# A hand-written schedule with shifted priorities: 207 parts of a four-layer network on one core

## The chip, the core and the metric

The kernel runs on one core of a Trainium2 chip. A core has four compute engines that each work through their own instruction list in order: PE (matrix multiplies, with its weight loads shown as PEld), DVE (vector work), ACT (activation functions and copies) and POOL (general vector work). SP here only issues DMA transfers. The engines run beside each other and wait for one another by semaphores. PE reads its operands from the on-chip memory SBUF and writes into PSUM[...].

The metric is the device time of one execution in microseconds (us). Shown are the median of three runs, and one profiled execution with its trace.

## What is computed

An input of 8 sequences x 256 tokens x 128 channels goes through six blocks, each with a normalisation in front and a residual sum behind:

```python
x = x + 0.5 * soft_moe(layernorm(x))
x = x + linear_attention(layernorm(x))
x = x + 0.5 * soft_moe(layernorm(x))       # the same weights
x = x + 0.5 * ternary_glu(layernorm(x))
x = x + favor_attention(layernorm(x))
x = x + 0.5 * ternary_glu(layernorm(x))    # the same weights
```

The soft mixture of experts (16 experts, 64 slots each, hidden width 256):

```python
logits   = einsum("bnd,esd->bnes", layernorm(x), slot_keys)
dispatch = softmax(logits, axis=tokens)
combine  = softmax(logits, axis=all_slots)
slots    = einsum("bnd,bnes->besd", layernorm(x), dispatch)
hidden   = gelu(slots @ Wg + bg) * (slots @ Wu + bu)
out      = einsum("bns,bso->bno", combine, hidden @ Wd + bd)
```

Linear attention has 16 heads of 8 channels with elu(x)+1 features; the favor attention has the same heads with 32 random exponential features. The glu block has silu(w1 x) * (w2 x) with width 512, then two 512 x 512 layers with gelu, then a projection back to 128. All numbers are float32.

## The kernel before

The eight sequences (called batches b) are split into two groups of four. Each group passes through the six blocks: dispatch for its four batches, 16 experts over all four batches at once, combine and linear attention for each batch, a second dispatch, experts and combine, then a glu for each pair of batches, favor attention for each batch, and a glu for each pair again, which stores the result.

Nothing is issued in that order. `macaron_kernel` first only describes the work: every call of `step` (many hundreds of them) adds a `Step` with a length in ns on each engine that could do it, the buffers and cells that it reads and writes, and a closure that issues the instructions. `Plan.place` (L97) then puts the steps in order with a small model: it takes again and again the step that can start first, over all engines that it may use; ties are broken by `s.key` (L136). A step can start when its inputs are done (plus a lag for the engine that made them), its engine is free, and there are free slots for the buffers that it is the first to use. `issue` (L168) runs the closures by the starts found. From then on each engine's list is fixed; on the chip only the semaphores count, and a step that comes late holds up all that stands behind it on its engine.

The key is the sum of the PE lengths of the steps described so far in a group (L86); the second group starts at 45,000 ns (`BEHIND`, L201). So of two steps that could start at once, the one nearer to the front of its group's work goes first, with the second group 45 us behind:

```python
late = self.TABLE if s.table and s.table != table else 0
rank = (at, s.key + 4 * late, s.number)
```

`late` is the time of loading another function table on ACT (exp, gelu or silu); a step that needs one is ranked behind others.

The places that are spoken of later:

- `normalized` (L348): statistics on DVE (L361, L362), the root on POOL (L367, L368), the subtraction and scaling on POOL or DVE (L374).
- `transposed` (L394): turns a tile on PE (L331), brought out of PSUM by a copy (L338 on ACT, L340 on DVE) or with gain and bias (L416 on ACT, L418 on DVE).
- `dispatch` (L498): four steps of logits (L511), copied to the buffer `comb`, with a running maximum on DVE (L528). Then for each half of the slots a token softmax: maximum on DVE (L542), exp with its sum on ACT (L550), reciprocal on DVE (L558), division on POOL (L563), turned on PE, and gathered into the slots (L584). Last, for the combine softmax: the maximum over slots (L603, turn, L614), spread by PE (L623), subtracted on POOL (L635), exp on ACT (L641).
- `experts` (L647): `fetch` loads an expert's weights (L660, L661; three buffers), `front` does two hidden steps (L675), gelu (L681) and the product (L686), `back` the down multiply (L705) and bias (L715).
- `combine` (L736): the multiply with the combine weights (L742).
- `linear` (L800): sums over tokens (L853), cut to blocks on DVE (L859, L864), used by the next multiply (L876).
- `hidden` (L931): a 512 x 512 layer of the glu on 256 + 256 rows with seven block products (L958) in place of eight, subtractions before them on POOL or DVE (L943), copies (L338), adds (L972) and gelus (L980) after. `glu` (L1009) has two of them, and the down multiply (L1055).
- `favor` (L1071): features (L1131, L1143 to L1148), exps (L1158), sums (L1192) and products (L1223).

Of the kernel before, what the change touches and what calls it, by code (L numbers as in the profile page):

```python
# [11 lines left out]
ALU = mybir.AluOpType  # L12
AX = mybir.AxisListType
P = 128


class Buf:
# [3 lines left out]
    def __init__(self, kind, shape):  # L21
        self.kind, self.shape = kind, shape
        self.left = 0
        self.slot = None
        self.home = None
# [22 lines left out]
class Plan:  # L48
# [7 lines left out]
    LAG = {"PE": 300, "ACT": 120, "DVE": 100, "POOL": 150, "SP": 2200}  # L56
    TABLE = 1300

    def __init__(self, slots):
        self.slots = slots  # L60
        self.steps = []
        self.writer, self.readers = {}, {}
        self.key = 0

    def step(self, engines, run, reads=(), writes=(), takes=(), table=None):
        s = Step(len(self.steps), engines, run, table, self.key)
        for c in reads:
            if c in self.writer:
                s.needs.add(self.writer[c])
        for c in writes:  # L70
            if c in self.writer:
                s.needs.add(self.writer[c])
            s.needs.update(self.readers.get(c, ()))
        for c in reads:
            self.readers.setdefault(c, set()).add(s)
        for c in writes:
            self.writer[c] = s
            self.readers[c] = set()
        s.needs.discard(s)
        for c in (*reads, *writes, *takes):  # L80
            b = c[0] if isinstance(c, tuple) else c
            if isinstance(b, Buf) and b not in s.bufs:
                s.bufs.append(b)
                b.left += 1
        self.steps.append(s)
        if "PE" in engines:  # L86
            self.key += engines["PE"]
        return s
# [88 lines left out]
def macaron_kernel(ctx: ExitStack, tc: tile.TileContext, i: dict, out: bass.AP):  # L177
# [26 lines left out]
    kinds = {  # L204
        "comb": (NJ * N, 9),
        "slots": (NJ * NB * 4 * S1, G),
        "k4": (1024, 6),
        "k2": (512, 7),
        "k1": (256, 14),
        "kv": (272, 6),  # L210
        "we": (6 * P + D, 3),
        "sm": (32, 40),
        "ps": (512, 8),
    }
    plan = Plan({k: n for k, (_, n) in kinds.items()})
    step = plan.step


# [31 lines left out]
    for h in range(2):  # L250
        part = slice(4 * h, 4 * h + 4)
# [9 lines left out]
    ng = load("norm_g", [P, 1])  # L261
# [54 lines left out]
    def act(n, pointers=False):  # L316
        return 160 + 0.83 * n + 100 * pointers

    def dve(n, extra=0):
        return 150 + 1.05 * n + extra  # L320

    def mms(*columns):
        return sum(2 * max(107, 0.84 * n) for n in columns)

    def flips(n):
        return 110 * n
# [21 lines left out]
    def normalized(tiles, twice=False):  # L348

        n = len(tiles)
        mv = Buf("sm", (P, 32))

        def stats(_):
            for t, (_, src, _, _) in enumerate(tiles):
                st = mv.ap[:, 8 + 6 * t : 14 + 6 * t]  # L360
                nc.vector.bn_stats(st, src())  # L361
                nc.vector.bn_aggr(mv.ap[:, 2 * t : 2 * t + 2], st)  # L362

        def root(_):
            v = mv.ap[:, 1 : 2 * n : 2]
            eps = EPS * EPS / (1.0 + EPS) if twice else EPS
            nc.gpsimd.tensor_scalar(v, v, eps, None, ALU.add)  # L367
            nc.gpsimd.tensor_tensor(v, v, power[:, 0:n], ALU.pow)  # L368

        step({"DVE": 400 * n}, stats, [t[2] for t in tiles], [mv], takes=[t[3] for t in tiles])  # L370
        step({"POOL": 600 + 160 * n}, root, [mv], [mv])
        for t, (dst, src, r, w) in enumerate(tiles):
            def apply(e, t=t, dst=dst, src=src):
                (nc.gpsimd if e == "POOL" else nc.vector).tensor_scalar(  # L374
                    dst(), src(), mv.ap[:, 2 * t : 2 * t + 1], mv.ap[:, 2 * t + 1 : 2 * t + 2],
                    ALU.subtract, ALU.mult,
                )

            step({"POOL": 800, "DVE": 360}, apply, [r, mv], [w])

    def norm(b, twice=False, y=None, at=0):

# [28 lines left out]
    def affinely(dst, src, r, w, n):  # L411


        def run(e):
            if e == "ACT":
                nc.scalar.activation(dst(), src(), AF.Identity, bias=nb, scale=ng)  # L416
            else:
                nc.vector.tensor_scalar(dst(), src(), ng, nb, ALU.mult, ALU.add)  # L418

        step({"ACT": act(n, True), "DVE": dve(n, 120)}, run, [*r, "ng"], w)  # L420


    def keys():
# [74 lines left out]
    def dispatch(b, sl):  # L498


        odd, q = b % 2, b % BG
        y = norm(b, True)
        yt = transposed(y, TT, True)
# [2 lines left out]
        for u in range(4):  # L506
# [19 lines left out]
            if u:  # L526
# [4 lines left out]

                step({"DVE": dve(2 * N)}, greater, [pl, pm, (comb, 0)], [pm])


        for h in range(2):
            mx = Buf("sm", (P, 16))
# [61 lines left out]
                lambda po=po: po.ap, [po], [(sl, j, q) for j in range(4 * h, 4 * h + 4)], 512,  # L598
            )


        def fold(_):
            nc.vector.tensor_tensor(pm.ap[:, 0], pm.ap[:, 0], pm.ap[:, 1], ALU.max)  # L603
# [43 lines left out]
    def experts(sl):  # L647
# [78 lines left out]

        got = {}
        for e in range(E + 1):
            if e < E:
                we = fetch(e)  # L730
                got[e] = (we, front(e, we))
            if e >= 1:
                back(e - 1, *got.pop(e - 1))
        return eo

    def combine(b, comb, sl, eo):  # L736
        q = b % BG
        po = ps_(TT, 256)
        for t in range(TT):
            def gather(_, t=t):  # L740
                for j in range(NJ):
                    mm(  # L742
                        po.ap[:, t, 0 : D + 1], comb.ap[:, j, ts(t, P)], eo()[:, j, q, 0 : D + 1],
                        start=(j == 0), stop=(j == NJ - 1),
                    )

            step(
                {"PE": mms(*[D + 1] * NJ)}, gather,
                [(comb, u) for u in range(4)] + [(sl, j, q) for j in range(NJ)], [(po, t)],
            )  # L750
        rc = Buf("sm", (P, TT))

        def add(_):
            nc.vector.reciprocal(rc.ap, po.ap[:, :, D])
            for t in range(TT):
                n = b * TT + t
                nc.vector.scalar_tensor_tensor(
                    x[:, n, :], po.ap[:, t, 0:D], rc.ap[:, t : t + 1], x[:, n, :],
                    ALU.mult, ALU.add,
                )  # L760

        step({"DVE": 900}, add, [(po, t) for t in range(TT)] + [("x", b)], [("x", b)], takes=[rc])
# [35 lines left out]


    def linear(b):  # L800
        yt = transposed(norm(b), TT)
        plus_bias(b, bproj)
        pk, pv = ps_(2, N), ps_(TT, D)
# [41 lines left out]

        step({"POOL": 110}, ones, [pv], [(v1, 1)])


        pkv = ps_(D + 1)

# [15 lines left out]
            )  # L866

        step({"PE": mms(D + 1, D + 1)}, sums, [kq, v1, (v1, 1)], [pkv], takes=[kv])
        step({"DVE": 500}, blocks, [pkv], [kv])
        po = ps_(TT, 256)  # L870
        rd = Buf("sm", (P, TT, H))
        oh = Buf("k1", (P, TT, D))
# [58 lines left out]
    def hidden(h, to, t4, w, wbufs):  # L931
# [9 lines left out]
        def sub(dst, a, b, r, w):  # L941
            def run(e):
                (nc.gpsimd if e == "POOL" else nc.vector).tensor_tensor(  # L943
                    dst(), a(), b(), ALU.subtract
                )

            step({"POOL": 1200, "DVE": 800}, run, r, w)

        sub(T(1), B(0, 1), B(0, 0), [(h, 0, 1), (h, 0, 0)], [(t4, 1)])
        sub(T(2), B(1, 1), T(1), [(h, 1, 1), (t4, 1)], [(t4, 2)])  # L950
# [58 lines left out]
    def glu(b, after):  # L1009
        if not held:  # L1010
            for name, scales, parts in (
                ("h1T", "hs1", [("slots", 7)]), ("h2T", "hs2", [("comb", 4), ("comb", 3)])
            ):
                bufs = [Buf(kind, (P, n, 2, 256)) for kind, n in parts]
                held.append(combined_weights(name, scales, bufs, b))
        y = Buf("k2", (P, 2 * TT, D))
        for k in range(2):
            norm(b + k, False, y, k * TT)
# [3 lines left out]
        for o in range(NO):  # L1022
# [21 lines left out]
            step({"ACT": act(512, True)}, silu, [pg], [si], table="silu")  # L1044
            step({"DVE": dve(512, 65)}, product, [pu, si], [(h, o // 2, k) for k in range(2)])
        for w in held:
            hidden(h, to, t4, *w)
            h, to = to, h
        for k in range(2):
            po = ps_(TT, D)  # L1050

            def down(_, k=k, po=po, h=h):
                for t in range(TT):
                    for c in range(NO):
                        mm(  # L1055
                            po.ap[:, t, :], h.ap[:, c // 2, k, c % 2, ts(t, P)], w3s[:, c, :],
                            start=(c == 0), stop=(c == NO - 1),
                        )

            def add(_, k=k, po=po):  # L1060
                xb = x[:, ts(b + k, TT), :]
                nc.vector.tensor_tensor(xb, po.ap, xb, ALU.add)

            step(
                {"PE": mms(*[P] * TT * NO)}, down, [(h, 0, k), (h, 1, k), "w3s"], [po]
            )
            step({"DVE": dve(N)}, add, [po, ("x", b + k)], [("x", b + k)])
            after(b + k)


    def favor(b):  # L1071
        yt = transposed(norm(b), TT)
        plus_bias(b, bo)
        pq, pv = ps_(2, N), ps_(TT, P)
# [33 lines left out]
        )  # L1108
        step({"POOL": 120}, ones, [pv], [(v1, 1)])


        pn = ps_(2, TT, H)

# [40 lines left out]
        for k in (1, 0):  # L1154
# [6 lines left out]
            if k:  # L1161
# [2 lines left out]

                step({"POOL": 2900}, eps, cells, cells)

        qt = lambda t: qk.ap.rearrange("p a b n -> p (a b n)").rearrange(
# [78 lines left out]
    def group(g):  # L1248
# [20 lines left out]
        for b in bs_[::2]:  # L1269
            glu(b, store)  # L1270

    keys()
    plan.key = 150000
    weights()
    for g in range(G):
        plan.key = BEHIND * g
# [64 lines left out]
```

## Time and profile before

| what | value |
|---|---|
| median of 3 runs | 789.29 us (788.82 to 789.86) |
| the profiled execution | 788.46 us |
| its span, first to last instruction | 786.8 us |
| PE clock granted | 1.0 of full speed |
| multiplies and transposes, as PE instructions | 4584 |
| first PE instruction starts | 7.21 us |
| last multiply ends | 783.45 us |
| table loads on ACT, 1283 ns each | 96 |
| DMA moved | 36.96 MB, mean 47 GB/s |

A float32 multiply stands in the trace as two PE instructions, a transpose as one. The busy time of an engine is the union of its instructions. A PE instruction's own duration (380 ns for 256 columns) is longer than the distance to the next one in a packed row, because instructions overlap in the array; what limits PE is that distance. In the row of forty slices each digit is the busy share of one slice of 19.7 us in tenths. In a timeline row, the first number is the start, the second the duration, and the bracket at the end gives the idle time of the engine ahead of it and what ended it.

### The profile page before, as it was taken

What the parts mean: (1) busy time and instruction counts of PE and PEld (TensorE: products, weight loads), DVE (VectorE), ACT (ScalarE), POOL (GpSimd) and SP (SyncE); (2) the same over time, 40 slices, a digit from 0 to 9 for tenths busy, and PEclk for the clock granted to TensorE, in tenths of its full rate; (3) what the DMA queues carried; (4) which work ended last, traced back from release to release, by engine and by line L of the source; (5) the groups of instructions that cost most, each with busy time, mean ns of one, the idle gap of its engine ahead of it and who ended that gap; (6) DMA issues with size and microseconds to landing.
All of it is one profiled execution on the core that took longest, in us unless ns stands there. A gap on an engine that the chain in (4) does not pass through costs nothing.

```text
span 786.8 us, 12435 instructions
## 1 busy us (share of the span) xinstructions
PE 759.1 (96%) x4584; PEld 630.9 (80%) x4584; DVE 536.7 (68%) x1170; ACT 458.3 (58%) x826; POOL 340.6 (43%) x365
## 2 busy tenths in 40 slices
PE   3899999999999999999999999999999999999997
PEld 2667787999887888878888987898787987778875
DVE  5899787478886887895664455447897488873242
ACT  2889889555894689895363324426475255633232
POOL 7998424323367545547722042234544323620001
PEclk9999999999999999999999999999999999999999
DMA  6101233313230122332523100000000000000000
GB/s 192 40 0 39 77 97 95 112 54 114 74 95 1 55 66 76 94 106 58 153 74 92 47 1 1 1 0 2 1 1 1 1 1 15 2 0 1 21 7 15
DMA packets 27580, 36.96 MB, mean 47 GB/s; under 512 B 3808, under 2 KB 18816, under 8 KB 27520
## 3 DMA queue, kind: packets, MB, share of 16 engines
q1 hardware_dynamic: 25968, 35.62, 15.4%
q8 instruction: 36, 0.59, 0.3%
q10 hardware_dynamic: 1488, 0.53, 0.3%
q14 instruction: 24, 0.20, 0.1%
q0 software_dynamic: 64, 0.03, 0.0%
HBM read 35.12 MB, written 1.05 MB: 46 GB/s over the span
## 4 chain that ended last, share of the span: by engine, by line
PE 87%; DVE 5%; POOL 4%; DMA 1%; issue 1%; ACT 1%; ACTq 0%; POOLq 0%; SPq 0%; DVEq 0%
PE ps L958 24%; PE ps L675 13%; PE ps L742 7%; PE ps L705 7%; PE ps L331 5%; PE ps L511 5%; PE ps L584 5%; PE ps L1030 4%; PE ps L1055 3%; PE ps L1027 3%; PE ps L1192 2%; POOL k L563 1%; PE ps L1131 1%; PE ps L1117 1%; PE ps L1223 1%; POOL sm L368 1%
## 5 line engine op out<-in xcount | busy, mean ns | idle before, releaser
L675 PE MATMUL ps<-slots,we 128*128 128x256 f32 x512 | 124.4, 380 | 0.0
L338 ACT COPY k<-ps 128x512 f32<-128x512 f32 (+1 forms) x97 | 50.5, 540 | 122.1 <-PE ps L958 74.3
L675 PEld LDWEIGHTS ps<-slots,we 128*128 128x128 f32 x512 | 93.0, 189 | 17.6 <-issue 6.0
L958 PE MATMUL ps<-comb,comb 128*128 128x256 f32 x448 | 104.6, 381 | 2.5 <-ACT k L338 1.7
L958 PE MATMUL ps<-comb,slots 128*128 128x256 f32 x448 | 103.4, 379 | 0.0
L563 POOL TENSOR_TENSOR k<-k,sm 128x1024 f32<-128x1024 f32 x32 | 61.0, 1908 | 85.8 <-DVE sm L558 85.7
L958 PEld LDWEIGHTS ps<-comb,comb 128*128 128x128 f32 x448 | 83.3, 190 | 16.2 <-ACT k L338 2.7
L958 PEld LDWEIGHTS ps<-comb,slots 128*128 128x128 f32 x448 | 83.9, 190 | 14.3 <-issue 3.6
L635 POOL TENSOR_TENSOR comb<-comb,k 128x1024 f32<-128x1024 f32 x32 | 75.8, 2386 | 19.4 <-DVE k L340 14.1
L681 ACT ACTIVATE k<-ps,bg 128x256 f32<-128x256 f32 x128 | 55.3, 473 | 41.3 <-PE ps L675 36.2
L331 PE MATMUL ps<-ident,k 128*128 128x128 f32 x408 | 61.7, 279 | 16.5 <-POOL k L374 9.1
L686 DVE SCALAR_TENSOR_TENSOR k<-ps,bu,k 128x256 f32<-128x256 f32 x128 | 56.9, 477 | 25.1 <-ACT k L681 24.2
L972 DVE TENSOR_TENSOR comb<-ps,k 128x512 f32<-128x512 f32 x48 | 33.0, 688 | 59.5 <-ACT k L338 30.1
L331 PEld LDWEIGHTS ps<-ident,k 128*128 128x128 f32 x408 | 48.8, 143 | 28.6 <-POOL k L374 10.9
L705 PEld LDWEIGHTS ps<-we,k 128*128 128x128 f32 x512 | 65.0, 191 | 7.5 <-issue 3.4
L715 DVE TENSOR_TENSOR slots<-ps,we 64x256 f32<-64x256 f32 x128 | 53.7, 420 | 25.0 <-PE ps L705 20.0
L705 PE MATMUL ps<-we,k 128*128 128x128 f32 x512 | 67.6, 275 | 0.8 <-DVE k L686 0.8
L550 ACT ACTIVATE k<-comb,sm 128x256 f32<-128x256 f32 x128 | 63.4, 498 | 5.8 <-DVE sm L542 3.4
L943 POOL TENSOR_TENSOR comb<-comb 128x512 f32<-128x512 f32 x16 | 25.1, 1570 | 92.8 <-ACT comb L980 56.2
L511 PE MATMUL ps<-k,seT 128*128 128x256 f32 x256 | 62.7, 384 | 0.7 <-ACT k L416 0.7
L742 PEld LDWEIGHTS ps<-slots,comb 128*128 128x128 f32 x512 | 59.6, 192 | 3.0 <-issue 2.6
L742 PE MATMUL ps<-slots,comb 128*128 128x129 f32 x512 | 60.8, 275 | 0.0
(143 smaller groups left out, 1413.1 us busy)
## 6 DMA issues: line engine op xcount, KB each, us to landing
we<-in_We SPq DMA_DIRECT2D x64, 384.0 KB, 3.1
we<-in_bd SPq DMA_DIRECT2D x64, 64.0 KB, 3.0
x<-in_L_attn_x SPq DMA_DIRECT2D x4, 256.0 KB, 5.9
comb<-in_h2T SPq DMA_DIRECT2D x4, 256.0 KB, 4.6
slots<-in_h1T SPq DMA_DIRECT2D x4, 256.0 KB, 6.3
out<-x SPq DMA_DIRECT2D x8, 128.0 KB, 1.7
k<-in_slot_embeds ACTq DMA_DIRECT2D x2, 256.0 KB, 6.1
k<-in_hs SPq DMA_DIRECT2D x2, 256.0 KB, 3.5
```

Of the source, the lines that this page charges most:

```text
L331: nc.tensor.transpose(po, src, ident)
L511: mm(pl.ap[:, j, :], seT[:, 2 * u + j, odd : odd + 2].rearrange("p k s -> p (k s)"), yt.ap, start=True, stop=True,)
L550: nc.scalar.activation(ex.ap[:, j, :], comb.ap[:, 4 * h + j, :], AF.Exp, bias=mx.ap[:, j : j + 1], accum_out=mx.ap[:, 4 + j : 5 + j],)
L563: nc.gpsimd.tensor_tensor(ex.ap, ex.ap, mx.ap[:, 8:12].unsqueeze(2).to_broadcast([P, 4, N]), ALU.mult)
L635: nc.gpsimd.tensor_tensor(raw, raw, mb.ap.unsqueeze(1).to_broadcast([P, 4, N]), ALU.subtract)
L675: mm(pe.ap[:, m, :], we.ap[:, ts(2 * m + c, P)], sl.ap[:, j, :, k::2, 0:S], start=True, stop=True,)
L681: nc.scalar.activation(ga.ap, pe.ap[:, 0, :], AF.Gelu, bias=bg[:, e, c : c + 1])
L686: nc.vector.scalar_tensor_tensor(ht.ap[:, c, :], pe.ap[:, 1, :], bu[:, e, c : c + 1], ga.ap, ALU.add, ALU.mult,)
L705: mm(po.ap[:, q, :], ht.ap[:, c, ts(q, P)], we.ap[:, ts(4 + c, P)], start=(c == 0), stop=(c == 1),)
L715: nc.vector.tensor_tensor(eo()[rows, j, (u ^ k) :: 2, 0:D], po.ap[rows], we.ap[rows, 6 * P :].unsqueeze(1).to_broadcast([S, NB, D]), ALU.add,)
L742: mm(po.ap[:, t, 0 : D + 1], comb.ap[:, j, ts(t, P)], eo()[:, j, q, 0 : D + 1], start=(j == 0), stop=(j == NJ - 1),)
L958: mm(bank.ap[:, o], w(k)[:, c, ts(o, P)], rhs().rearrange("p (c n) -> p c n", c=2)[:, c, :], start=(start and o + c == 0), stop=(stop and ...
```

## The change

Three things are changed, all in how the plan is made.

First, the work is cut into 207 parts. `Plan.part` is called at the head of each part: one for each third of a dispatch, one for each expert (the front of one and the back of the one before), one for each combine, two for each linear attention, three for each favor attention, four for each glu, and one each for the first load, the keys and the weights. All steps described within a part get the part's shift added to their key.

Second, the 207 shifts themselves, a table of numbers in units of 100 ns, from -2546 to 1488; 125 of them are negative. They were found by a search. A negative shift moves a part forward among steps that could start at the same time.

Third, eight step lengths of the model take other values, set to those of the trace: the shortest multiply, the statistics and the scaling of a normalisation, the affine copy on ACT, the blocks of the linear attention and the subtractions of the hidden layers.

```diff
+SHIFTS = (
+    -1227, -613, -401, -68, -58, -18, -64, -450, -1382, -1020, -424, -281, -256, -288, -233,
...
+    -923, 156,
+)
...
-    def __init__(self, slots):
+    def __init__(self, slots, shifts=()):
         self.slots = slots
+        self.shifts, self.parts = shifts, -1
+        self.part()
...
+    def part(self):
+
+        self.parts += 1
+        self.shift = 100 * self.shifts[self.parts] if self.parts < len(self.shifts) else 0
+
     def step(self, engines, run, reads=(), writes=(), takes=(), table=None):
-        s = Step(len(self.steps), engines, run, table, self.key)
+        s = Step(len(self.steps), engines, run, table, self.key + self.shift)
+        s.part = self.parts
...
-    plan = Plan({k: n for k, (_, n) in kinds.items()})
+    plan = Plan({k: n for k, (_, n) in kinds.items()}, SHIFTS)
...
-        return sum(2 * max(107, 0.84 * n) for n in columns)
+        return sum(2 * max(112, 0.84 * n) for n in columns)
...
-        step({"DVE": 400 * n}, stats, [t[2] for t in tiles], [mv], takes=[t[3] for t in tiles])
+        step({"DVE": 455 * n}, stats, [t[2] for t in tiles], [mv], takes=[t[3] for t in tiles])
...
-            step({"POOL": 800, "DVE": 360}, apply, [r, mv], [w])
+            step({"POOL": 840, "DVE": 430}, apply, [r, mv], [w])
...
-        step({"ACT": act(n, True), "DVE": dve(n, 120)}, run, [*r, "ng"], w)
+        step({"ACT": act(n, True) + 90, "DVE": dve(n, 120)}, run, [*r, "ng"], w)
...
-        step({"DVE": 500}, blocks, [pkv], [kv])
+        step({"DVE": 730}, blocks, [pkv], [kv])
...
-            step({"POOL": 1200, "DVE": 800}, run, r, w)
+            step({"POOL": 1450, "DVE": 950}, run, r, w)
...
     def dispatch(b, sl):
+        plan.part()
         odd, q = b % 2, b % BG
...
         for e in range(E + 1):
+            plan.part()
             if e < E:
                 we = fetch(e)
                 got[e] = (we, front(e, we))
```

The other calls of `plan.part()` are of the same form.

## The prediction

> **What bounds the kernel now.** I read the busy shares first, then the forty slices, then what the matrix engine (PE) waits for, then three short stretches of the timeline.
>
> ```profile
> PE 759.1 (96%) x4584; PEld 630.9 (80%) x4584; DVE 536.7 (68%) x1170; ACT 458.3 (58%) x826; POOL 340.6 (43%) x365
> ...
> PE   3899999999999999999999999999999999999997
> ...
> POOL 7998424323367545547722042234544323620001
> ```
>
> PE is busy nearly everywhere; only the first three slices and the last one are not full. So the room is small, and I size it by a floor: what the PE instructions take when packed. Pieces of the chain of waits give the start-to-start times: 1.73 us for 8 multiplies of 256 columns (0.216 each), 1.72 for 4 of 512 (0.430), 1.79 for 16 of 128 (0.112), 1.75 for 16 transposes (0.109). Times the counts: 1712 of 256 columns, 370; 256 of 512, 110; 1568 of 128 to 144, 176; 472 transposes, 51; 192 narrow ones at 0.107, 21; the 384 tiled ones by their busy time, 18. That makes about 745 us, and the diff changes none of these instructions. The span is 786.8, so about 41 us are not packed: 7.2 before the first transpose, 3.4 after the last multiply, 31 between.
>
> Where are the 31? The first expert multiply (L675) starts at 65.59. Before it stand 96 logit multiplies (20.7), 94 transposes (10.2), 28 gathers (12.0) and 16 small ones (1.8): 44.8 us of work in 65.6, so **20.8 us are lost by then**. The stretch view and the timeline of POOL say why (columns of the first: PE, PEld, DVE, ACT, POOL busy with counts, then clock, DMA share, GB/s):
>
> ```profile
> 18.00:66.00 48.00, 44.27 (x220) 32.80 (x219) 43.14 (x72) 41.73 (x115) 47.49 (x36) 1.00 0.06 21
> 66.00:142.00 76.00, 74.47 (x407) 59.86 (x407) 58.70 (x121) 66.92 (x124) 36.00 (x28) 1.00 0.32 90
> ```
>
> ```profile
> 40.21 4.88 POOL L635 TENSOR_TENSOR comb<-comb,k 128x1024 f32<-128x1024 f32 x2
> ...
> 51.76 4.88 POOL L635 TENSOR_TENSOR comb<-comb,k 128x1024 f32<-128x1024 f32 x2
> 56.59 3.75 POOL L563 TENSOR_TENSOR k<-k,sm 128x1024 f32<-128x1024 f32 x2
> ```
>
> From 18 to 66 us POOL has 0.5 us of idle time. It divides the dispatch softmax (L563, 1.9 us), which the experts need, and between these it subtracts maxima for the combine softmax (L635, a pair 4.7 to 4.9 us), which nothing needs before the combine; a third pair runs from 30.89. **The experts wait behind POOL work that is not urgent.** From 66 us on the losses are single waits, 17 us in all with group changes and the end.
>
> **The change, part by part.** No instruction's size changes; the numbers in the steps only change the order and which engine takes a step. In the order of the changed program's instructions I counted:
>
> *Start.* Before its first expert multiply stand 72 logits (15.6), 72 transposes (7.8), 24 gathers (10.3), 4 small ones (0.4): 34.2 us. POOL has one pair of L635 instead of three before the last division that this multiply needs. Up to the first division little moves (26.4 us now). Then 6 divisions (11.4), one normalisation (0.8), the w3 scaling (1.9) and one L635 pair (4.8): 18.9, so about 45 us. From a division's end to the multiply lie two transpose steps (0.9), a copy (0.7), the gather (0.9), the affine (0.8): 3.5 with handovers; now the seventh division ends at 58.4 and the multiply comes 7.1 later. So the first expert starts between 48.5 and 52.1, with 14.3 to 17.9 lost instead of 20.8: a gain of 2.9 to 6.4, I take 5. The deferred L635 are late next; POOL is busy 36.0 of the next 76 us, which covers them.
>
> *ACT.* That gain must survive ACT, 66.9 of 76 us busy from 66 to 142, where the 32nd gelu runs. Up to it the new order holds 24 table loads instead of 20, 5 fewer affines (L416, 0.7 each), 2 fewer copies (0.6), one exp less (1.05). A rule of the Trainium skill speaks against the loads: "ScalarE: Activation LUTs", What ACT_TABLE_LOAD costs, charges a switch with its 1283 ns and a drain of 1380 ns. The row shows only the load:
>
> ```profile
> 119.06 0.47 ACT L681 ACTIVATE k<-ps,bg 128x256 f32<-128x256 f32 x1 [0.39 <-DVE k L528]
> 119.55 1.28 ACT L641 ACT_TABLE_LOAD   x1
> ...
> 120.84 1.06 ACT L641 ACTIVATE comb<-comb 128x1024 f32<-128x1024 f32 x1
> ```
>
> The load starts 0.02 after the gelu ends and the exp 0.01 after the load. By the row: +5.1 -3.5 -1.2 -1.05, about -0.6 us; by the rule four times 2.66, so +4.9. I take the row. At the 32nd expert step PE has 115.0 us of packed work behind it now and 111.6 in the new order, so if ACT kept its pace to that point the start would lose 3.4 instead. ACT has 9 us of idle time there, and its first gelu has 8 fewer exps and 6 fewer L641 ahead of it, so I deduct 1: **start +4, between -3.4 and +6.4**.
>
> *Middle.* Twelve waits after 66 us and before the tail add to 6.2 us, each with some 0.16 hidden in a modelled end: 8. The largest:
>
> ```profile
> 249.78 4.67 POOL L635 TENSOR_TENSOR comb<-comb,k 128x1024 f32<-128x1024 f32 x2 [0.49 <-DVE k L340]
> ...
> 252.58 1.95 DVE L864 TENSOR_SCALAR kv<-m,ps 128x16 f32<-128x16 f32 x1
> ...
> 254.58 0.76 PE L876 MATMUL ps<-kv,k 128*128 128x144 f32 x4 [1.69 <-DVE kv L864]
> ```
>
> L864 takes 0.23 us in the median and 1.95 here; it ends as POOL's L635 does. A new length (500 to 730) cannot foresee such a block, but more PE work between producer and consumer covers it: for the eight L853-L876 pairs it was 0.44 to 1.79 us, and becomes 1.3 to 9.9 with five above 2. Half of the 8: **+4**, between 0 and 8.
>
> *New waits.* Hidden to down (L675 to L705) needs a gelu (0.47), the product (0.48) and about 0.4 of handovers, 1.35. The PE work between was under 2.3 us at 3 of 64 experts and is at 12 now (least 1.55). None has a table load directly ahead of its second gelu, but a late ACT or DVE shows at once. Also, DVE gives 9 of its 39 subtracts (L943) to POOL: 9 x 1.4, some 13 us more on POOL. "SBUF — State Buffer", Who interferes with whom, says that a DVE instruction with two SBUF inputs and a POOL instruction that reads SBUF block each other. L603 agrees (0.42 median, 2.28 at most). By the rule up to 13 us of DVE blocking; by the row one of twelve waits came of it beside 340 us of POOL, so 13 us more add 0.1. Together I take **-1**, between 0 and -10 (all 12 late by 0.85).
>
> *Tail.* The last glu runs alone, and its hidden layer waits four times:
>
> ```profile
> 768.41 1.99 PE L958 MATMUL ps<-comb,comb 128*128 128x256 f32 x8 [0.45 <-DVE comb L943]
> 770.76 1.99 PE L958 MATMUL ps<-comb,comb 128*128 128x256 f32 x8 [0.36 <-POOL comb L943]
> 773.49 1.99 PE L958 MATMUL ps<-comb,comb 128*128 128x256 f32 x8 [0.73 <-ACT k L338]
> 776.16 1.13 PE L958 MATMUL ps<-comb,comb 128*128 128x256 f32 x4 [0.68 <-ACT k L338]
> ```
>
> 2.2 us and 0.6 of hidden ends. In the new order the second hidden layers of two glus alternate up to the last four down steps, so one covers the other's adds and gelus: **+2.5**, between 0 and 2.9. The last add and store stay. SP's expert weights change places only with neighbours; DVE waited 0.8 us in all for one, PE never.
>
> **Sum.** 4 + 4 - 1 + 2.5 = 9.5 us off the profiled execution's 788.5 (span 786.8): 779.0. The runs' median is 0.8 above it: **779.8**. A change under 0.2%, 1.6 us, cannot be told from none.
>
> **Rivals.**
> *All room is used*: 6.4 + 8 + 2.9 = 17.3, some 772. For it: each loss above has a visible cause that order can mend. Against: blocks between POOL and DVE fall by chance. Chance 0.13.
> *The start gives nothing*, because POOL, full to 66 us and ACT still 88% busy to 142, only hand the delay on: 9.5 - 4 - 1 = 4.5, about 785. For it: the 3.4 above. Chance 0.17; a sixth of it within 0.2%.
> *Slower: the tight hand-offs of the experts.* If ACT or DVE comes 0.85 us late at all 12, the middle loses 10, and with the start at -3.4: 3.4 + 10 - 4 - 2.5 = 7 us, about 796. It decides once more than ten of the twelve are late with no gain at the start. For it: one engine order, fixed ahead, cannot give way. Against: 1.77 us at one expert shows no wait now. Chance 0.12.
> *The order does not change*: ruled out, its instructions stand differently on every engine.
>
> The forecast itself has 0.58. Faster 0.85, same 0.03, slower 0.12. The range, 770.5 to 789, takes in the first two rivals; some 0.13 lies above it and 0.06 below.
>
> **What will show it.** First expert multiply at 48 to 52 us; POOL with one L635 pair before it; PE's waits after 66 us under 6 us in total; no four waits in the last 20 us; still 41 us minus the gain unpacked. I am wrong if PE waits for L681 or L686 at many experts, or if the first expert moves and the group's last one does not.

## The result, and the profile after

| | before | changed |
|---|---|---|
| median of the runs, us | 789.06 (788.22 to 789.86) | 777.68 (776.96 to 779.44) |
| ratio to before, 95% interval | | 0.9859 (0.9839 to 0.9879) |
| span of the profiled execution, us | 786.8 | 775.8 |
| first expert multiply at, us | 65.59 | 54.95 |
| waits of PE in the view of waits after 66 us, us | 8.4 | 1.9 |
| table loads on ACT | 96 | 91 |

The change takes 11.4 us off the median and 11.0 off the span. Lines of the changed kernel are 25 to 41 higher: L331 is L356, L374 is L399, L563 is L590, L635 is L663, L675 is L703, L958 is L990.

The page of the changed kernel, busy time first, then the forty slices (19.4 us each):

```profile
PE 754.0 (97%) x4584; PEld 631.6 (81%) x4584; DVE 528.2 (68%) x1156; ACT 450.4 (58%) x824; POOL 351.2 (45%) x376
...
PE   2999999999999999999999999999999999999998
```

The view of PE's waits is complete in five rows (waiter, releaser: us in total, times, longest):

```profile
PE ps L356 <- POOL k L399: 13.6, 3, 11.3
PE ps L537 <- ACT k L441: 1.6, 2, 1.2
PE ps L356 <- POOL k L590: 1.4, 1, 1.4
PE ps L537 <- ACT seT L477: 0.9, 1, 0.9
PE ps L841 <- ACT k L363: 0.5, 1, 0.5
```

The first, second and fourth row lie before 30 us. After that PE waits twice in 745 us, at 80.9 us for a division (L590) and at 177.9 us for a copy (L363). Before, this view had fifteen rows with 26 waits.

To see where the gain lies I use the prediction's floor as a curve: the start of a PE instruction, less the packed time of all PE work ahead of it, is what PE has lost by then. It can only rise, apart from some 0.5 us of reading error. (The expectations below use a first reckoning of the same curve, up to 1 us lower late in the run.) Each column is what the stretch loses:

| stretch, us | before | changed | gain |
|---|---|---|---|
| 0 to 30 | 18.8 | 20.3 | -1.5 |
| 30 to 66 | 2.0 | 0.5 | 1.5 |
| 66 to 142 | 2.5 | 2.1 | 0.4 |
| 142 to 760 | 10.6 | 2.9 | 7.7 |
| 760 to the last multiply | 3.4 | 0.1 | 3.3 |
| after it | 3.4 | 3.7 | -0.3 |

**The start gives nothing; the gain is made after 142 us.** Two times show that more directly: before has its first expert multiply 10.6 us later, but has done 44.8 us of packed work by then and the changed kernel 34.2, so both have lost 20.8. One execution is little for that, but three more runs below plan the start as the changed kernel does and have lost 20.5, 20.9 and 22.9 by 66 us, and a second execution of the start before has lost 20.7 (the last run of the table below).

At the end, the timeline of PE in the changed kernel has no bracket in the last 12 us, where before had four:

```profile
763.16 1.89 PE L990 MATMUL ps<-comb,comb 128*128 128x256 f32 x8
764.88 1.95 PE L1090 MATMUL ps<-w3T,comb 128*128 128x128 f32 x16
766.67 1.89 PE L990 MATMUL ps<-comb,comb 128*128 128x256 f32 x8
768.40 3.73 PE L1090 MATMUL ps<-w3T,comb 128*128 128x128 f32 x32
```

Each start follows the one before by the packed time (1.73 and 1.79): a down step of one glu stands between the last hidden products of the other.

And at the start the changed kernel has a wait that it did not have before. The timeline of DVE, first in the changed kernel:

```profile
7.96 0.29 DVE L386 BATCH_NORM_STATS2 sm<-x 128x6 f32<-128x128 f32 x1 [7.96 <-DMA x<-in_L_attn_x]
```

and in the kernel before:

```profile
3.86 0.29 DVE L361 BATCH_NORM_STATS2 sm<-x 128x6 f32<-128x128 f32 x1 [3.86 <-DMA x<-in_L_attn_x]
```

The shifts put batch 2 first (its first part has -1020, that of batch 0 only -68). Batch 2 comes with the second load of x. The plan gives one landing time to all of x (7000 ns, L245), so in the plan this order costs nothing.

### The profile page after: what moved, and what is told of

The parts are those of the page before. It is cut to its first block, busy times and chain, and to the rows that moved or that the text cites. A ratio compares the mean times of both kernels' runs of the same rounds, so it can differ in the third digit from the quotient of the medians.

```text
span 775.8 us, 12408 instructions
## 1 busy us (share of the span) xinstructions
PE 754.0 (97%) x4584; PEld 631.6 (81%) x4584; DVE 528.2 (68%) x1156; ACT 450.4 (58%) x824; POOL 351.2 (45%) x376
## 3 DMA queue, kind: packets, MB, share of 16 engines
q10 hardware_dynamic: 1488, 0.53, 0.3%
## 4 chain that ended last, share of the span: by engine, by line
PE 95%; POOL 1%; DVE 1%; DMA 1%; ACT 0%; SPq 0%; issue 0%; POOLq 0%
PE ps L990 25%; PE ps L703 14%; PE ps L772 7%; PE ps L733 7%; PE ps L611 7%; PE ps L537 7%; PE ps L356 6%; PE ps L1090 4%; PE ps L1060 4%; PE ps L1063 4%; PE ps L1230 2%; PE ps L1168 1%; PE ps L1261 1%; PE ps L820 1%; PE ps L651 1%; PE ps L1154 1%
## 5 line engine op out<-in xcount | busy, mean ns | idle before, releaser
L363 ACT COPY k<-ps 128x512 f32<-128x512 f32 (+1 forms) x99 | 51.6, 533 | 128.2 <-PE ps L990 79.7
L703 PE MATMUL ps<-slots,we 128*128 128x256 f32 x512 | 121.0, 380 | 0.0
L703 PEld LDWEIGHTS ps<-slots,we 128*128 128x128 f32 x512 | 93.8, 189 | 16.6 <-issue 4.3
L990 PE MATMUL ps<-comb,comb 128*128 128x256 f32 x448 | 102.8, 380 | 0.0
L990 PE MATMUL ps<-comb,slots 128*128 128x256 f32 x448 | 101.9, 381 | 0.0
L663 POOL TENSOR_TENSOR comb<-comb,k 128x1024 f32<-128x1024 f32 x32 | 75.1, 2365 | 57.3 <-ACT k L577 29.6
L990 PEld LDWEIGHTS ps<-comb,slots 128*128 128x128 f32 x448 | 83.8, 190 | 13.4 <-issue 1.9
L990 PEld LDWEIGHTS ps<-comb,comb 128*128 128x128 f32 x448 | 83.4, 190 | 11.8 <-issue 1.4
L975 POOL TENSOR_TENSOR comb<-comb 128x512 f32<-128x512 f32 x20 | 30.6, 1530 | 123.9 <-ACT comb L1012 73.3
L590 POOL TENSOR_TENSOR k<-k,sm 128x1024 f32<-128x1024 f32 x32 | 60.6, 1903 | 35.7 <-DVE sm L585 34.3
L356 PE MATMUL ps<-ident,k 128*128 128x128 f32 x408 | 60.1, 276 | 15.1 <-POOL k L399 13.6
L714 DVE SCALAR_TENSOR_TENSOR k<-ps,bu,k 128x256 f32<-128x256 f32 x128 | 57.3, 477 | 22.7 <-ACT k L709 21.7
L709 ACT ACTIVATE k<-ps,bg 128x256 f32<-128x256 f32 x128 | 56.4, 473 | 26.1 <-PE ps L703 25.2
L356 PEld LDWEIGHTS ps<-ident,k 128*128 128x128 f32 x408 | 49.0, 143 | 26.0 <-POOL k L399 14.6
L743 DVE TENSOR_TENSOR slots<-ps,we 64x256 f32<-64x256 f32 x128 | 53.8, 421 | 20.3 <-PE ps L733 17.4
L733 PE MATMUL ps<-we,k 128*128 128x128 f32 x512 | 65.4, 275 | 0.0
L1012 ACT ACTIVATE comb<-comb 128x512 f32<-128x512 f32 x48 | 29.9, 628 | 54.2 <-DVE comb L1004 54.1
```

The lines of the kernel that those rows point to most:

```text
L356: nc.tensor.transpose(po, src, ident)
L590: nc.gpsimd.tensor_tensor(ex.ap, ex.ap, mx.ap[:, 8:12].unsqueeze(2).to_broadcast([P, 4, N]), ALU.mult)
L663: nc.gpsimd.tensor_tensor(raw, raw, mb.ap.unsqueeze(1).to_broadcast([P, 4, N]), ALU.subtract)
L703: mm(pe.ap[:, m, :], we.ap[:, ts(2 * m + c, P)], sl.ap[:, j, :, k::2, 0:S], start=True, stop=True,)
L709: nc.scalar.activation(ga.ap, pe.ap[:, 0, :], AF.Gelu, bias=bg[:, e, c : c + 1])
L714: nc.vector.scalar_tensor_tensor(ht.ap[:, c, :], pe.ap[:, 1, :], bu[:, e, c : c + 1], ga.ap, ALU.add, ALU.mult,)
```

## The experiments

Four questions: which half of the change works, where, why the start gives nothing, and what the waits are that went. In the runs limited to a part of the plan, the two lines added move all later lines by two.

| run | time, us | ratio (95%) | lost at 66 | 66 to 400 | 400 to the end |
|---|---|---|---|---|---|
| before | 788.5 to 789.1 | | 20.8 | 8.1 | 8.4 |
| changed | 777.68 | 0.9859 (0.9839 to 0.9879) | 20.8 | 3.1 | 2.0 |
| lengths only | 791.72 | 1.0038 (1.0023 to 1.0053) | 21.9 | 9.4 | 7.7 |
| shifts to 66 us | 795.65 | 1.0086 (1.0069 to 1.0103) | 20.5 | 14.8 | 7.8 |
| shifts from 600 us | 788.95 | 1.0001 (0.9992 to 1.0009) | 23.5 | 9.3 | 4.2 |
| shifts to 400 us | 783.04 | 0.9931 (0.9917 to 0.9945) | 22.9 | 3.3 | 7.6 |
| shifts halved | 809.85 | 1.0264 (1.0241 to 1.0286) | 23.7 | 25.7 | 6.3 |
| one old length | 791.41 | 1.0029 (1.0016 to 1.0042) | 20.9 | 16.6 | 2.0 |
| before, subtraction later | 794.45 | 1.0070 (1.0058 to 1.0083) | 18.8 | 16.5 | 8.1 |
| changed, first pair first | 775.66 | 0.9836 (0.9820 to 0.9851) | 18.5 | 3.2 | 2.0 |
| the same, small loads later | 774.70 | 0.9822 (0.9807 to 0.9837) | 18.0 | 3.2 | 1.9 |
| before, block in another form | 786.45 | 0.9969 (0.9958 to 0.9981) | 20.7 | 6.6 | 8.0 |

### The lengths without the shifts

```diff
-    plan = Plan({k: n for k, (_, n) in kinds.items()}, SHIFTS)
+    plan = Plan({k: n for k, (_, n) in kinds.items()})
```

> The changed kernel with all shifts left out: only the eight new step lengths act. Theory A (the shifts make the gain; the lengths alone just shuffle the plan): no less than 785 us, and the time that PE loses between 142 us and the end stays above 9 us (before 13.1, changed kernel 2.0). Theory B (a model with true lengths plans without waits): 776 to 781 us, and under 5 us lost after 142.

791.72 us, slightly slower than before, and 15.7 us lost after 142. Theory A holds: true lengths in the model do not by themselves avoid waits. The other half, all shifts with all old lengths, was not run: `Plan.place` then finds no step that can start, because there are too few buffers free.

### The shifts, limited to a stretch of the plan

The shift is kept beside the key and added only for choices at such times (here up to 66 us; in the two others from 600 us, and up to 400 us):

```diff
-        s = Step(len(self.steps), engines, run, table, self.key + self.shift)
+        s = Step(len(self.steps), engines, run, table, self.key)
+        s.shift = self.shift
...
-                    rank = (at, s.key + 4 * late, s.number)
+                    shift = s.shift if at < 66000 else 0
+                    rank = (at, s.key + shift + 4 * late, s.number)
```

> New lengths; the shifts count only for choices made before 66 us of the plan, so the start is that of the changed kernel and the rest is planned without shifts. Theory A (the start gives nothing): PE has lost 20 to 21 us at 66 us, as before and as in the changed kernel, and the time is within 4 us of the run with the lengths only. Theory B (the start does give 3 to 5 us, hidden in the profile by a late load): the time is 3 to 5 us below the run with the lengths only.

795.65, against 791.72 with the lengths only (3.9 us, just inside theory A's 4); at 66 us it has lost 20.5, as the changed kernel. No gain is hidden in the start. What follows without shifts happens to be worse than the run with the lengths only (14.8 against 9.4 us up to 400; some 1.7 of it is a stretch at a lower clock, see the last section).

> New lengths; the shifts count only from 600 us of the plan on, so up to there it is the run with the lengths only. Theory A (two glus side by side at the end cover each other): the time is 2 to 4 us below the run with the lengths only, all of it lost after 600 us there and not here. Theory B (the tail's gain needs the state that the earlier shifts leave): within 1 us of it.

788.95, 2.8 us below the lengths only. From 600 us to the last multiply it loses 2.6 us, the other 6.2. So 3.6 come from the shifts at the end alone, although they were found for another beginning. (At 66 us it had lost 1.6 more than the lengths only, with the same plan: about 1.0 of it by 30 us, most of the rest in a stretch at a lower clock, see the last section.)

> The changed kernel up to 400 us of the plan; from there on the shifts count no more. Theory A (each stretch has its own gain, which its own shifts make): up to 400 us PE has lost 23 us, as in the changed kernel, and from there to the end it loses 6 to 8, as in the run with the lengths only (7.1), so 782 to 785 us. Theory B (a good first half leaves a good state): it loses under 3 us after 400, under 780.

783.04, inside theory A's 782 to 785. From 66 to 400 us it loses what the changed kernel loses, and then what the lengths only lose. By 66 us it has lost 22.9, though, 2.1 more than the changed kernel with the same plan, and its profiled execution took 785.07, the longest of its four. The timeline of PE shows why, first in the changed kernel, then here:

```profile
22.45 5.45 PE L537 MATMUL ps<-k,seT 128*128 128x256 f32 x24 [1.16 <-ACT k L441]
```

```profile
22.88 7.10 PE L539 MATMUL ps<-k,seT 128*128 128x256 f32 x24 [0.90 <-ACT k L443]
```

In every run here PE's first logits start 0.43 us apart in place of 0.216, while the granted clock is shown as 1.00. In the changed kernel this ends before the row of 24, here a few multiplies into it. So what a start loses differs by up to 2 us between executions of one plan. The four waits of before are back at its end, to 0.01 us (timeline of PE):

```profile
765.00 1.99 PE L992 MATMUL ps<-comb,comb 128*128 128x256 f32 x8 [0.45 <-DVE comb L977]
767.35 1.99 PE L992 MATMUL ps<-comb,comb 128*128 128x256 f32 x8 [0.35 <-POOL comb L977]
770.07 1.99 PE L992 MATMUL ps<-comb,comb 128*128 128x256 f32 x8 [0.73 <-ACT k L365]
772.74 3.72 PE L992 MATMUL ps<-comb,comb 128*128 128x256 f32 x16 [0.68 <-ACT k L365]
```

The gain is local: against the lengths only, the shifts up to 400 us make 6.1 us of it after the start (9.4 to 3.3) and those behind 400 us 5.7 (7.7 to 2.0), and a good first half leaves nothing over for the second.

### Do the shifts point somewhere, or do they fit one plan?

```diff
-        self.shift = 100 * self.shifts[self.parts] if self.parts < len(self.shifts) else 0
+        self.shift = 50 * self.shifts[self.parts] if self.parts < len(self.shifts) else 0
```

> All shifts at half their size, lengths new. Theory A (the shifts fit one plan and are no trend): nearer to the run with the lengths only than to the changed kernel, over 783 us. Theory B (they move the parts in a direction that is good in itself): about half of the way or more, under 783 us.

809.85, 18 us worse than no shifts. Half of the way is not half of the gain; it is the worst plan of all here. In it PE even waits 2.4 us for an expert's weights, which it never did before.

```diff
-        step({"DVE": 730}, blocks, [pkv], [kv])
+        step({"DVE": 500}, blocks, [pkv], [kv])
```

> The changed kernel with one length put back, 730 to 500 ns for the blocks of the linear attention, all shifts in place. Theory A (the shifts hold for exactly one plan): the plan takes another course after the first linear attention, near 165 us, PE loses 6 us or more from there to the end where the changed kernel loses 1.6, and the time is over 783 us. Theory B (the lengths only cover their own waits): only waits at that step come back, at most 2 us, so under 780.

791.41. The curve is that of the changed kernel up to 200 us, soon after the first such block; then it loses more, some 13 us more up to 400 (1.7 of them a lower clock, see the last section). The block itself (L896) makes little of it, 0.9 us. The view of PE's waits names many others, among them:

```profile
PE ps L651 <- DVE sm L642: 2.9, 2, 2.4
...
PE ps L733 <- DVE k L714: 1.6, 2, 1.1
...
PE ps L356 <- DVE k L631: 1.3, 1, 1.3
PE ps L908 <- DVE kv L896: 0.9, 2, 0.7
```

One length, 230 ns longer, is worth 13.7 us here, because the greedy plan takes another course and the 207 shifts no longer meet the choices for which they were found. Lengths and shifts are one thing: neither has a gain of its own to be added up.

What each half is for can be read from the plan itself, since `Plan.place` also computes when its last step ends (`span`), from the kernel file alone. That end is 773.6 us for the changed kernel, 781.6 with shifts to 400 us, 790.1 from 600 us, 792.5 with the lengths only, 795.9 to 66 us and 802.6 with the shifts halved: the order of the measured times, and at most 7.3 us from them. With the old lengths it is 776.2 for the kernel before, and with the one old length 784.0, 12.9 and 7.4 us too early. So the new lengths make the plan nearly true, and most of what the shifts gain or lose is already in the plan. That the search worked on this plan is likely, but not on record.

### Why the start gives nothing

The prediction said that the experts wait behind POOL's subtractions. Before, with only these put later, for the first four batches:

```diff
-        (15000, ["weights"]),
+        (15000, ["weights"]), (52000, ["later"]),
...
-            step({"POOL": 2400}, less, [mb, *half], half)
+            later = ["later"] if plan.key < 40000 else []
+            step({"POOL": 2400}, less, [mb, *half, *later], half)
```

> The kernel before with one thing changed: the plan may place the subtractions for the combine softmax (L635) of the first four batches only after 52 us, so that all seven divisions that the first expert needs stand ahead of them on POOL. Theory A (the prediction's: the experts wait behind POOL): the first expert starts at 48 to 56 us and PE has lost 15 to 18 us at 66 us instead of 20.8. Theory B (18.8 us are already lost at 30 us, and from there PE finds other work): the first expert does not start before 60 us, PE has lost at least 18.8 at 66 us, and the start is worth at most 2 us.

The first expert starts at 60.81, and the seventh division is done at 53.3, with idle POOL before it. The timeline of POOL:

```profile
41.48 1.90 POOL L563 TENSOR_TENSOR k<-k,sm 128x1024 f32<-128x1024 f32 x1 [1.25 <-DVE sm L558]
45.95 1.90 POOL L563 TENSOR_TENSOR k<-k,sm 128x1024 f32<-128x1024 f32 x1 [2.57 <-PE ps L584]
51.41 1.89 POOL L563 TENSOR_TENSOR k<-k,sm 128x1024 f32<-128x1024 f32 x1 [3.57 <-DVE sm L558]
53.27 14.16 POOL L635 TENSOR_TENSOR comb<-comb,k 128x1024 f32<-128x1024 f32 x6
```

With the subtractions gone, POOL waits twice for DVE's reciprocal and once for a gather of PE. The loss is 18.8 at 30 us and 18.8 at 66: theory B to the digit. The 18.8 belong to the first 30 us, the loads, the normalisations, the slot keys and the multiplies at half pace; after that PE was never short of work for long. And what was put off comes back as a block of 14 us on POOL. PE waits twice soon after, until 69.33 and 71.93 us, both times for DVE; one of DVE's instructions there (L603) took 1.51 us beside these subtractions, in place of 0.42. In all the run is 5.9 us slower than before on the same chip.

What the first 30 us hold can be mended. First the order of the loads, in the changed kernel:

```diff
-    nc.sync.dma_start(x_of(0, 2), xin[:, 0:2])
+    nc.sync.dma_start(x_of(2, 2), xin[:, 2:4])
...
-    for q in range(1, 4):
+    for q in (0, 2, 3):
```

> The changed kernel with the loads of x exchanged: the pair of batches 2 and 3, which its shifts put first, is loaded first, and batches 0 and 1 second. The order on PE, DVE, ACT and POOL is the same. Theory A (the first normalisation waits 4 us for the second load, which the plan believes to land with the first): first statistics near 4 us instead of 8.0, first logits near 15.0 instead of 16.9, and 1 to 2 us off the time, so 775.5 to 776.7. Theory B (the slot embeddings, landing at 8.4 to 9.1, set the start anyway): under 0.7 us.

775.66: 2.0 us below the changed kernel's median. The two intervals overlap, so the times alone don't prove it, but the first statistics start at 3.90 and the first logits at 14.81, as theory A said, and 18.5 are lost at 66 us, less than in all four executions with the changed start (20.5 to 22.9). The embeddings then land at 8.32:

```profile
3.90 0.29 DVE L386 BATCH_NORM_STATS2 sm<-x 128x6 f32<-128x128 f32 x1 [3.90 <-DMA x<-in_L_attn_x]
...
7.00 0.21 DVE L452 TENSOR_SCALAR gs<-slot_g,scale 128x1 f32<-128x1 f32 x1 [2.20 <-DMA scale<-in_scale]
...
8.32 0.29 DVE L386 BATCH_NORM_STATS2 sm<-k 128x6 f32<-128x128 f32 x1 [0.93 <-DMA k<-in_slot_embeds]
```

DVE waits for them, so they were asked for first:

```diff
-    sg = load("slot_g", [P, 1], eng=nc.scalar)
-    sb = load("slot_b", [P, 1], eng=nc.scalar)
-    sc = load("scale", [P, 1], i["scale"].partition_broadcast(P), eng=nc.scalar)
+    sg = load("slot_g", [P, 1])
+    sb = load("slot_b", [P, 1])
+    sc = load("scale", [P, 1], i["scale"].partition_broadcast(P))
```

> The kernel with the exchanged pairs of x, and the three small loads of the slot norm (gain, bias, scale) issued by SP instead of ahead of the slot embeddings on ACT's queue, so that the embeddings are asked for 1.4 us earlier. Theory A (the landing of the embeddings, 8.3 us, sets the first logits at 14.8): first logits 1 to 1.5 us earlier, PE has lost 17 to 17.5 us at 66 us instead of 18.5, time 774 to 775. Theory B (DVE, which takes the small loads first in its order, or the transfers themselves, hold it): under 0.5 us, or slower where the later pairs of x, which are asked for 1.4 us later, come late.

774.70, the fastest here. The first logits come at 13.70, 1.1 earlier, but the loss at 66 us falls only by 0.5, to 18.0, where theory A had 17 to 17.5. PE spends the rest at half pace: the first eight logits take 3.78 us and the six transposes behind them 1.49, in the run before 3.56 and 0.82. The interval overlaps that run's, so this second step is likely, not proved.

### What one of the lost waits was

Before, the largest single wait in the middle was 1.69 us for L864, which took 1.95 us in place of 0.23 while POOL ran a subtraction.

```diff
-            nc.vector.tensor_scalar(
-                kv.ap[:, D : D + H], m16, pkv.ap[:, D : D + 1], None, ALU.mult
-            )
+            nc.vector.tensor_tensor(
+                kv.ap[:, D : D + H], m16, pkv.ap[:, D : D + 1].to_broadcast([P, H]), ALU.mult
+            )
```

> The kernel before with one instruction of the linear attention in another form: the 16 column block (L864) as a tensor_tensor with one operand in SBUF and one in PSUM, in place of the tensor_scalar with its operand in SBUF and a pointer in PSUM. Theory A (the tensor_scalar was held by a port that POOL had): at 252 us it takes 0.2 to 0.4 us instead of 1.95, PE no longer waits 1.69 us for it, and the time is 1 to 2 us below before. Theory B (DVE was held by something else): it still takes over 1 us there.

Timeline of this run around the place, POOL, DVE and PE:

```profile
249.75 4.69 POOL L635 TENSOR_TENSOR comb<-comb,k 128x1024 f32<-128x1024 f32 x2 [0.49 <-DVE k L340]
...
252.55 0.16 DVE L864 TENSOR_TENSOR kv<-m,ps 128x16 f32<-128x16 f32 x1
...
252.77 0.76 PE L876 MATMUL ps<-kv,k 128*128 128x144 f32 x4
```

POOL's pair lies at the same place to 0.03 us, and the DVE instruction beside it takes 0.16 us. PE goes on at 252.77, not at 254.58. The time falls by 2.5 us (theory A had 1 to 2), to a ratio of 0.9969. Theory A holds: the form of the DVE instruction, not its work, was what POOL's subtraction held up. It agrees with what "SBUF — State Buffer" of the Trainium skill says under Who interferes with whom: a `tensor_scalar` can take the port that it shares with POOL, a DVE instruction with one SBUF input outside such a mode does not. That the first form took that port is not shown; the run shows only that it was held and the other was not.

## Why the prediction was right, and where it was not

Predicted were 779.8 us and 9.5 us of gain; it is 777.68 and 11.0 in the profiled execution, inside the range. That the sum came so near is luck in part: the start was put 4 us too high, and the middle with its new waits 5 us too low.

- **The start, +4: wrong; it gave 0.0 up to 66 us and 0.4 up to 142.** The step that failed is "20.8 us are lost by then", put down as a whole to POOL. The stretch view began at 18 us and showed POOL full, and from a full engine I concluded that it was the bound. But PE was busy 44.3 of the same 48 us. Of the 20.8 lost, 18.8 were lost by 30 us, and an estimate of 14.3 to 17.9 in the new order asked for more than could be won after it. The first expert at 54.95, where I had 48.5 to 52.1, says little: it was moved ahead of other work, and PE was packed either way. Putting the subtractions off alone gained 2.0 and then cost 8, of which 3.4 are a lower clock (last section).
- The start's second half was not seen: the shifted batch waits for the second load, 4 us, of which 2.0 to 2.3 reach the end (the run with the pair first). The two halves cancel, -1.5 up to 30 us and +1.5 after.
- **ACT, -1, and its table loads: no loss.** From 52 to 142 us ACT was busy 84.9 of 90, and PE named it once after 30 us, 0.5 us.
- **The middle, +4 less 1 for new waits: too small; it gave 7.7 from 142 to 760 us, and no new waits.** I took half of 8 us of waits, since I held them for chance that an order made ahead can't avoid. It avoided all but two: with the 0.4 before 142 us the gain is 8.1, as much as all of the 8. The twelve tight hand-offs to the down multiply (1.55 us and more) held: PE waits for L709 or L714 nowhere in the changed kernel. That the whole gain is so narrow, though, shows in the one old length. POOL's busy time grew by 10.6 us (340.6 to 351.2), yet DVE was hardly held more: of its subtractions comb<-comb,comb (L943, now L975; 0.69 us alone) 9 took 1.3 us or more beside POOL before and 10 do now, and PE waits for none of these.
- **The tail, +2.5: right in its cause, and a little more than its range of 0 to 2.9: 3.3.** Run from 600 us on alone, the shifts gave 3.6.
- The weight of blocks between POOL and DVE was right in kind (one wait in twelve) and shown by the other form of L864. But that wait is no case of two SBUF inputs, under which I counted it: L864 reads one operand from SBUF and one from PSUM (`kv<-m,ps`).

The rival "slower" had its place: the same kind of plan, one length off or the shifts halved, is at 791 and 810.

## What to carry to other kernels

Loss on the bounding engine adds up and never comes back: draw it as a curve over time, and let no estimate of a later stretch ask for more than that stretch lost. An engine that is full beside a PE that is nearly full is no bound until PE is seen waiting for it. Priorities found by a search against a greedy plan are tied to every number in it: change one length and search again; and give the model the landing time of each load, or the plan can put first what comes last. Before a loss at the start is compared, more than one execution is needed: here one plan's start differed by up to 2 us.

## What was not expected of the hardware

Waits close together can cost more than themselves. In the run with the subtraction later two of them, 2.15 and 1.50 us, end at 69.33 and 71.93 us, and the granted clock falls (stretch view of PE: start and end, length, PE busy, clock, DMA share, GB/s):

```profile
70.00:75.00 5.00, 3.50 (x10) 0.59 0.00 0
75.00:80.00 5.00, 5.00 (x28) 0.73 0.23 76
```

At 0.59 and 0.73 over 5 us each, 5 x 0.41 + 5 x 0.27 = 3.4 us of full clock are missing, about as much as the waits (3.65). From 80 us on the clock is at 1.00 again.

But such waits do not always lower it. The lengths only and the shifts from 600 us have the same plan at 60 us and the same two waits ahead of four gathers, 1.46 and 0.34 us in the first, 1.45 and 0.35 in the second. Timeline of the gathers and stretch view, first the lengths only:

```profile
59.17 1.98 PE L611 MATMUL ps<-k,k 128*128 128x512 f32 x4 [0.34 <-DVE k L365]
60.00:65.00 5.00, 4.29 (x20) 1.00 0.01 3
```

then the shifts from 600 us:

```profile
60.10 3.32 PE L613 MATMUL ps<-k,k 128*128 128x512 f32 x4 [0.35 <-DVE k L367]
60.00:65.00 5.00, 4.89 (x15) 0.66 0.01 3
```

There 5 x 0.34 = 1.7 us of full clock are missing. The runs with the shifts to 66 us (357 to 362 us) and with the one old length (355 to 360 us) show a 0.66 over 5 us too, behind waits of 1.19 and 0.52 us in the first and behind one of 2.35 in the second. In the kernel before, the clock stays at 1.00 in every stretch through single waits of up to 1.7 us. What decides it no run here shows, nor why the first logits run at half pace while the clock is shown as 1.00.
